# Transposed contexts from DRAM for the last layer, and the transpose of the router's shares a turn later

## The chip, the cores and the metric

The kernel runs on one NeuronCore of a Trainium2 chip. The metric is the device time of one execution in microseconds (us), the median of several runs; lower is better. The core has five engines with instruction queues of their own: TensorE (PE) multiplies matrices and transposes tiles into PSUM; VectorE (DVE), ScalarE (ACT) and GpSimd (POOL) work element by element; SyncE (SP) issues nearly all DMAs here. Everything is float32.

## The reference

A sequence of four layers on `x` of shape (128, 64, 128): 128 batches of 64 tokens with 128 channels. `cond` has one row of 128 for each batch, and `ctx` has the shape of `x`.

```
x = L0(x, cond, ctx)   # self attention, cross attention to ctx, MLP
x = L1(x, ctx, cond)   # cross attention to a normed ctx
x = L2(x, cond, ctx)   # self attention, cross attention to a normed ctx, MLP
x = L3(x, cond, ctx)   # one-head attention to ctx, then three experts with a router
```

All attention has 16 heads of width 8, except that of layer 3:

```
# L0, cross attention: the context enters without a norm
k, v = split(ctx @ kv_w + kv_b)
x = x + attend(ln(x) @ q_w + q_b, k, v) @ ca_proj_w + ca_proj_b

# L3
nx = layer_norm(x, gamma, beta)
weights = softmax((nx @ Wq) @ (ctx @ Wk).T * 128 ** -0.5)
evidence = weights @ (ctx @ Wv)
combined = concat(nx, evidence, anchor)              # anchor: cond, the same for all tokens of a batch
probs = softmax(combined @ router_W + router_b)      # three experts
h = silu(combined @ e_w1[e] + e_b1[e])               # e = 0, 1, 2
routed = sum_e probs[e] * (h @ e_w2[e] + e_b2[e])
g = sigmoid(silu(combined @ gate_w1 + gate_b1) @ gate_w2 + gate_b2)
out = x + g * (routed @ out_w + out_b)
```

Two places of it bear on the change: the cross attention of layer 0 and layer 3 both need the raw context with channels on the partitions, that is, transposed.

## The kernel before, in words

**Tiling.** The 8192 tokens are cut into 16 groups (`NST`) of 512, eight batches each. A group of `x` is a tile of 128 partitions by 4 by 128 (`xs[s]`) and stays in SBUF throughout. A transposed group is a tile of 128 channels by 512 tokens, made by `transposed`: four PE transposes of 128x128 into one PSUM bank (L296), which ACT or DVE then copies to SBUF.

**Stages.** Five attentions over 16 groups each make 80 items, run in two pipelines (`attend`): first L0's self and cross attention, then L1's and L2's two. An MLP stage (`mlp`) follows each pipeline, and layer 3 (`layer_3`) ends the kernel. The order on every engine is the order in which the program is written out: `tc.manual_schedule()`. Each engine, SP's queue too, works strictly in that order. Neighbouring stages overlap: the last steps of one and the first "heads" of the next are called in turn.

**One item of attention.** `prepare` is a generator in eight pieces. For cross attention they are: load the context `c` (L345), statistics of `x`, norm, transposed context `cm` (L332, in L0 a plain ACT copy of the transposes), transposed `x`, keys (with POOL's `kbd`), queries, values. `scores`, `turned` and `weighted` make the attention in halves. `finish` has four pieces:

- the sums of the softmax go from the tile `o` to DRAM (`sums`, L486) and back in another shape (`rc`, L491), and half of `o` is moved to other partitions (L494)
- DVE takes the reciprocal (L496); it goes to DRAM (`recs`, L498) and comes back spread over the partitions (`rb`, L500)
- POOL multiplies: `oT` (L503), and adds a bias to `x`
- PE projects: `py` (L509), and DVE adds it to `x`

In one step, the context's transposes of an item are written just ahead of the second piece of `finish` of the item four places earlier, so that on SP a DMA issued with them stands just ahead of `recs`.

**Layer 3.** The products of the weights that don't depend on the data are made beside the MLP of layer 2. Each group then passes these functions: `load` (the context `c` and the statistics), `norm` (POOL), `nx` (transposes and affine), `context` (transposed context `cT`), `queries` and `score`, `weights` (ACT's exponential, DVE's sum and reciprocal, POOL's product into `pd`, L914), `turn_weights` (transposes of `pd`), `evidence`, `router`, `logits`, `shares` (softmax over the experts, `pr`, L962), `turn_shares` (one PE transpose of `pr`, L968, and ACT's copy `prT`, L970), seven times `hidden` (two matmuls each, L980 and L981), `gate`, four times `output`, one for each 128 tokens (L1012; L1015 uses `prT`), and `store`.

A turn `a` does the hidden layers of group `a`, while groups `a + 1` and `a + 2` come nearer and `a - 1` is finished. The turn's list is its order. Four places matter:

- it starts with `norm`, then `hidden(a, 6)`, then `turn_weights(a + 1)`
- `router(a + 1)` comes after `hidden(a, 3)`, and `queries(a + 2)` after `hidden(a, 4)`
- it ends with `output(a, 0)`, `shares(a + 1)`, `weights(a + 2)`, `turn_shares(a + 1)`
- `output(a, 1)` to `output(a, 3)` run in the next turn

Ahead of the turns lie seven heads, called between the last turns of the MLP, and a `bridge` that brings group 0's shares. Router, logits and shares use one PSUM buffer in turn (`ps`). The tiles `cT` and `acc` of layer 3 lie in the buffers of `cm` and `y`, two each.

Of the kernel before, what the change touches and what calls it, by code (L numbers as in the profile page):

```python
# [9 lines left out]
F32 = mybir.dt.float32  # L10
AF = mybir.ActivationFunctionType
ALU = mybir.AluOpType
# [3 lines left out]
P = 128  # L16
NST = 16
# [3 lines left out]
NT = TT * P  # L21
# [38 lines left out]
def tile_kernel(ctx: ExitStack, tc: tile.TileContext, a: dict, out: bass.AP):  # L60
    nc = tc.nc
    V, S, G, T = nc.vector, nc.scalar, nc.gpsimd, nc.tensor
# [3 lines left out]
    def const(shape, name):  # L66
        return cp.tile(shape, F32, tag=name, name=name)
# [3 lines left out]
    out_d = out.rearrange("b n c -> (b n) c").rearrange("(s t p) c -> s p t c", t=TT, p=P)  # L71
# [21 lines left out]
    xs = [const([P, TT, P], f"x{s}") for s in range(NST)]  # L93
# [16 lines left out]
    for name, n in (("L0_xcond_ca_proj_b", P), ("L1_xcond_bp", P), ("L2_xcond_b_cproj", P), ("L3_xcond_router_b", 3)):  # L110
        t = const([P, n], name)
# [11 lines left out]
    dp = ctx.enter_context(tc.tile_pool(name="dp", bufs=1, space=bass.MemoryType.DRAM))  # L123
# [163 lines left out]
    def stats_of(pool, src, eps):  # L287
        mv = pool.tile([P, TT, 2], F32, tag="mv", name="mv")
        stats(pool, src, mv)
        return mv, inv_std(pool, mv, eps)  # L290

    def transposed(psum, src):

        ps = psum.tile([P, 512], F32, tag="mm", name="psT")
        for t in range(TT):
            T.transpose(ps[:, ts(t, P)], src[:, t, :], ident)  # L296
        return ps

    def modulated(pool, ps, name, scale, shift, s, tag="xm"):
        xm = pool.tile([P, NT], F32, tag=tag, name=tag)  # L300
        V.tensor_tensor(by_batch(xm), by_batch(ps), mod(name, scale, s), ALU.mult)
        G.tensor_tensor(by_batch(xm), by_batch(xm), mod(name, shift, s), ALU.add)
        return xm
# [16 lines left out]
    def normed_by_pool(pool, src, mv, rs, tag):  # L320
        nmu = pool.tile([P, TT], F32, tag="nmu" + tag, name="nmu")
        G.tensor_scalar(nmu, mv[:, :, 0], -1.0, 0.0, ALU.mult, ALU.add)
        xn = pool.tile([P, TT, P], F32, tag=tag, name=tag)
        for t in range(TT):
            G.tensor_scalar(  # L325
                xn[:, t, :], src[:, t, :], nmu[:, t : t + 1], rs[:, t : t + 1], ALU.add, ALU.mult
            )
        return xn

    def copied(pool, ps, tag):  # L330
        t = pool.tile([P, NT], F32, tag=tag, name=tag)
        S.copy(t, ps)  # L332
        return t

    turn = [0]

    def prepare(pools, at):

        pool, psum = pools[:2]
        s, layer = at["s"], at["layer"]  # L340
        eps = 1e-5 if layer == "L1c" else 1e-6
        cross = layer[2] == "c"
        if cross:
            c = pool.tile([P, TT, P], F32, tag="c", name="c", bufs=3)
            nc.sync.dma_start(c, ctx_d[s])  # L345
        yield
        mv, rs = stats_of(pool, xs[s], eps)
        yield
        xn = normed_by_pool(pool, xs[s], mv, rs, "xn")
        if cross:  # L350
            cn = c
            if layer != "L0c":
                cn = pool.tile([P, TT, P], F32, tag="cn", name="cn", bufs=1)
                for t in range(TT):
                    S.activation(
                        cn[:, t, :], c[:, t, :], AF.Identity,
                        bias=ctx_nb[eps][:, s, t : t + 1], scale=ctx_rs[eps][:, s, t : t + 1],
                    )
        yield
        if layer == "L1c":  # L360
            kv_in = modulated_by_act(pool, transposed(psum, cn), "L1_xcond_Wss_kv", 0, 1, s, "cm")
        elif cross:
            kv_in = copied(pool, transposed(psum, cn), "cm")
        else:
            q_in = kv_in = modulated_by_act(pool, transposed(psum, xn), at["wmod"], 1, 0, s)
        yield
        if not cross:
            pass
        elif layer == "L1c":
            q_in = modulated(pool, transposed(psum, xn), "L1_xcond_Wss_q", 0, 1, s)  # L370
        else:
            q_in = copied(pool, transposed(psum, xn), "xm")
        yield


        pk = psum.tile([P, 512], F32, tag="mm", name="pk")
        T.matmul(pk, at["wk"], kv_in, start=True, stop=True)  # L377
        kT = pool.tile([P, NT], F32, tag="kT", name="kT")
        S.activation(kT, pk, AF.Identity, bias=at["bk"])  # L379
        i = turn[0] % 2  # L380
        turn[0] += 1
        vbd = vbds[i]
        kbd = pool.tile([P, 4, NB, L], F32, tag="kbd", name="kbd")
        for j in range(4):
            G.tensor_scalar(  # L385
                kbd[:, j], by_batch(kT), mask[:, j : j + 1], 1.0, ALU.mult, ALU.mult
            )
        yield
        pq = psum.tile([P, 512], F32, tag="mm", name="pq")
        T.matmul(pq, at["wq"], q_in, start=True, stop=True)  # L390
        qT = pool.tile([P, NT], F32, tag="qT", name="qT")
        S.activation(qT, pq, AF.Identity, bias=at["bq"])
        yield

        wv_pair = at["wv"].rearrange("p (i j d) -> p j i d", j=2, d=HD)
        pvv = psum.tile([P, NB, L], F32, tag="mm", name="pvv")
        for b in range(NB):
            for j in range(2):
                T.matmul(  # L399
                    pvv[ts(j, L), b, :], kv_in[:, ts(b, L)], wv_pair[:, j],  # L400
                    start=True, stop=True,
                )
        pv4 = pvv.rearrange("p b (i d) -> p b i d", d=HD)
        S.copy(vbd[0:L, :, :, 0:HD], pv4[0:L])
        S.copy(vbd[L:P, :, :, HD : 2 * HD], pv4[L:P])
        at.update(qT=qT, kbd=kbd, vbd=vbd)
# [445 lines left out]
    def layer_3():  # L852

        pmm = pools[1]
# [6 lines left out]
        def sb(shape, tag, bufs=2):  # L861
            of = pools[0] if tag in shared else l3_pool[0]
            return of.tile(shape, F32, tag=shared.get(tag, tag), name=tag, bufs=bufs)
# [5 lines left out]
            d["mv"], d["rs"] = stats_of(l3_pool[0], xs[s], 1e-5)  # L869

        def norm(d):
            d["xn"] = normed_by_pool(l3_pool[0], xs[d["s"]], d["mv"], d["rs"], "xn")

        def nx(d):
# [3 lines left out]
                d["nx"], ps, AF.Identity, bias=col("L3_xcond_ln_beta"),  # L878
                scale=col("L3_xcond_ln_gamma"),
            )  # L880

        def context(d):
            ps = transposed(pmm, d["c"])
            d["cT"] = sb([P, NT], "cT")
            S.copy(d["cT"], ps)

        def queries(d):
            ps = mm("pq")
# [132 lines left out]
                )  # L1021
            V.tensor_add(acc, po[:, 3, :], acc)  # L1022

        def store(d):
            acc = d["acc"]
            G.tensor_tensor(acc, acc, d["g"], ALU.mult)  # L1026
            G.tensor_tensor(acc, acc, xs[d["s"]], ALU.add)
            nc.sync.dma_start(out_d[d["s"]], acc)

        ds = [dict(s=s) for s in range(NST)]  # L1030

        def go(f, j, *more):
            if 0 <= j < NST:
                f(ds[j], *more)

        heads = [
            lambda: (go(load, 0), go(load, 1)),
            lambda: go(norm, 0),
            lambda: (go(nx, 0), go(context, 0), go(norm, 1)),
            lambda: (go(queries, 0), go(score, 0), go(load, 2)),  # L1040
            lambda: (go(weights, 0), go(nx, 1), go(context, 1), go(norm, 2)),
            lambda: (go(turn_weights, 0), go(queries, 1), go(score, 1)),
            lambda: (go(evidence, 0), go(load, 3)),
        ]
# [1 line left out]
        def bridge():  # L1046
            go(router, 0)
            go(weights, 1)
            go(logits, 0)
            go(shares, 0)  # L1050
            go(turn_shares, 0)

        def turn(a_):
            b_, c_ = a_ + 1, a_ + 2
            return [
                lambda: go(norm, c_ + 1),
                lambda: go(hidden, a_, 6),
                lambda: go(turn_weights, b_),
                lambda: go(output, a_ - 1, 1),
                lambda: go(hidden, a_, 0),  # L1060
                lambda: go(nx, c_),
                lambda: go(output, a_ - 1, 2),
                lambda: go(hidden, a_, 1),
                lambda: go(evidence, b_),
                lambda: go(output, a_ - 1, 3),
                lambda: go(store, a_ - 1),
                lambda: go(hidden, a_, 2),
                lambda: go(context, c_),
                lambda: go(hidden, a_, 3),
                lambda: go(router, b_),  # L1070
                lambda: go(hidden, a_, 4),
                lambda: go(queries, c_),
                lambda: go(hidden, a_, 5),
                lambda: go(logits, b_),
                lambda: go(score, c_),
                lambda: go(load, c_ + 2),
                lambda: go(gate, a_),
                lambda: go(output, a_, 0),
                lambda: go(shares, b_),
                lambda: go(weights, c_),  # L1080
                lambda: go(turn_shares, b_),
            ]

        return heads, bridge, [turn(j) for j in range(NST + 1)]
# [127 lines left out]
```

## Time and profile before

| | |
|---|---|
| time, median of three runs | 1814.87 us (1810.33 to 1819.31) |
| profiled execution: its own time | 1817.44 us |
| profiled execution: span of the instructions | 1815.7 us, mean granted clock of TensorE 0.975 |
| first pipeline (L0's attentions) | up to about 460 us |
| second pipeline (L1, L2) | about 570 to 1230 us |
| layer 3's turns | from 1350 us |
| from 1350 us to the end: PE, DVE, ACT, POOL busy | 407.4, 196.7, 188.7, 108.5 of 466 us, granted clock 0.93 |
| from 265 to 400 us (L0's cross attention): the same | 133.6, 121.8, 96.3, 92.7 of 135 us, granted clock 0.99 |

How to read it. The page gives busy times of each engine and, in 40 slices, its busy share in tenths; the row PEclk is the share of its full clock that PE was granted. In the waits, a row says which engine and line waited for which, for how long in all, how often, and the longest. In the timeline a row has the start and the length in us, engine, line, operation, tiles written and read, and in brackets the idle time before it and what ended it. In the windows a row has the stretch, its length, the busy time of PE, PE's weight loads, DVE, ACT and POOL with the number of instructions, then the granted clock, the share of the DMA engines and GB/s.

### The profile page before, as it was taken

To read this page: it belongs to the slowest core of one execution; us is meant where nothing else is said; L and a number is where in the kernel's file an instruction comes from. 1 tells how busy PE (TensorE), PEld (TensorE's weight loads), DVE (VectorE), ACT (ScalarE), POOL (GpSimd) and SP (SyncE) were. 2 spreads that over 40 slices of the span, in tenths; PEclk is the share of its full clock that TensorE was granted. 3 is DMA by queue.
4 is the path that set the end of the run, shared out by engine and by line. 5 is a ranking of instruction groups with operands and counts; after the bars stand their busy time and mean duration, and the time that the engine had idled before them with its cause. 6 is when DMAs were issued, how large, how long until landed. Compare 5 with 4: busy or idle time off the path is not lost. (4 is left out here: it accounts for less than half of the span.)

```text
span 1815.7 us, 64689 instructions
## 1 busy us (share of the span) xinstructions
PE 1648.6 (91%) x27756; PEld 1097.2 (60%) x27756; DVE 1248.5 (69%) x2281; ACT 1085.2 (60%) x1864; POOL 1028.0 (57%) x1671
## 2 busy tenths in 40 slices
PE   5999899998999888899998899989998989898987
PEld 3666567775444666676666677755545656555555
DVE  4899789996545888899898899964534344444443
ACT  4877667775335877778777788853344344444443
POOL 5677676666888566677777666666522222222211
PEclk9999999999999999999999999999999899899999
DMA  7233332221111122113333322111000000000000
GB/s 201 63 84 90 89 90 63 64 55 51 42 56 29 36 54 57 46 46 83 82 89 98 83 64 69 52 43 55 1 6 18 13 24 15 21 24 13 18 7 18
DMA packets 149949, 95.78 MB, mean 53 GB/s; under 512 B 35301, under 2 KB 132511, under 8 KB 149663
## 3 DMA queue, kind: packets, MB, share of 16 engines
q1 hardware_dynamic: 148874, 91.42, 18.4%
q8 instruction: 218, 3.57, 0.8%
q14 instruction: 68, 0.56, 0.1%
q10 hardware_dynamic: 789, 0.23, 0.1%
HBM read 71.41 MB, written 9.70 MB: 45 GB/s over the span
## 5 line engine op out<-in xcount | busy, mean ns | idle before, releaser
L425 DVE TENSOR_REDUCE mx<-sc 128x32 f32<-128x2048 f32 x160 | 365.9, 2287 | 81.0 <-PE sc L418 80.9
L447 ACT ACTIVATE eT<-pp 128x1024 f32<-128x1024 f32 x320 | 330.2, 1032 | 110.2 <-PE pp L443 110.2
L427 DVE TENSOR_TENSOR e<-sc,mx 128x2048 f32<-128x2048 f32 x160 | 366.6, 2291 | 5.5
L443 PEld LDWEIGHTS pp<-ident,e 64*128 64x128 f32 x5120 | 185.9, 140 | 202.4 <-issue 82.0
L385 POOL TENSOR_SCALAR kbd<-kT,mask 128x512 f32<-128x512 f32 x320 | 214.9, 690 | 59.8 <-ACT kT L379 59.2
L443 PE MATMUL pp<-ident,e 64*128 64x64 f32 x5120 | 230.0, 230 | 19.7 <-ACT eT L447 14.4
L325 POOL TENSOR_SCALAR xn<-x,nmu,rs 128x128 f32<-128x128 f32 x512 | 221.7, 446 | 13.4
L418 PE MATMUL sc<-kbd,qT 32*64 32x256 f32 x5120 | 181.1, 390 | 21.7 <-DVE e L427 20.2
L635 ACT ACTIVATE h<-ph,vec 128x512 f32<-128x512 f32 x128 | 87.3, 687 | 162.7 <-PE ph L634 162.5
L503 POOL TENSOR_TENSOR oT<-o,rb 128x512 f32<-128x512 f32 x80 | 101.8, 1273 | 145.2 <-DMA sums<-o 31.6
L460 PE MATMUL po<-eT,vbd 128*32 128x64 f32 x10240 | 176.9, 221 | 0.0
L987 ACT ACTIVATE h<-h 128x512 f32<-128x512 f32 x112 | 70.5, 630 | 168.2 <-DVE h L983 149.3
L983 DVE TENSOR_TENSOR h<-ph,ab 128x512 f32<-128x512 f32 x112 | 77.3, 690 | 133.6 <-PE ph L981 133.3
L460 PEld LDWEIGHTS po<-eT,vbd 128*32 128x32 f32 x10240 | 151.0, 110 | 12.2 <-DVE mv L276 0.8
L284 POOL TENSOR_TENSOR rs<-rs,nhalf 128x4 f32<-128x4 f32 x128 | 130.2, 1017 | 10.7
L418 PEld LDWEIGHTS sc<-kbd,qT 32*64 32x64 f32 x5120 | 98.3, 132 | 57.5 <-issue 33.7
L1019 DVE SCALAR_TENSOR_TENSOR acc<-po,pr,acc 128x128 f32<-128x128 f32 x128 | 44.9, 351 | 115.2 <-ACT acc L1017 112.9
L1026 POOL TENSOR_TENSOR acc<-acc,g 128x512 f32<-128x512 f32 x16 | 20.3, 1268 | 181.8 <-DVE acc L1022 135.5
L379 ACT ACTIVATE kT<-pk,vec 128x512 f32<-128x512 f32 x80 | 55.0, 687 | 111.1 <-PE pk L377 111.1
L283 POOL TENSOR_SCALAR rs<-mv 128x4 f32<-128x4 f32 x128 | 25.3, 198 | 156.5 <-DVE mv L276 142.2
L468 ACT COPY o<-po 128x512 f32<-128x512 f32 x160 | 95.5, 597 | 24.9 <-POOL oT L503 11.0
L274 DVE BATCH_NORM_STATS2 st<-x 128x6 f32<-128x128 f32 x512 | 110.3, 278 | 0.0
(257 smaller groups left out, 3109.9 us busy)
## 6 DMA issues: line engine op xcount, KB each, us to landing
rb<-recs SPq DMA_DIRECT2D x80, 256.0 KB
c<-in_ctx_dram SPq DMA_DIRECT2D x80, 256.0 KB
o<-o SPq DMA_DIRECT2D x320, 32.0 KB
gt<-gate_L_xcond_sa_proj_w SPq DMA_DIRECT2D x64, 128.0 KB
gt<-gate_L_xcond_W_proj SPq DMA_DIRECT2D x64, 128.0 KB
sums<-o SPq DMA_DIRECT2D x320, 8.0 KB
x<-in_x_dram SPq DMA_DIRECT2D x16, 256.0 KB
out_dram<-acc SPq DMA_DIRECT2D x16, 256.0 KB
```

The lines of the kernel that those rows point to most:

```text
L274: V.bn_stats(st[:, t, :], src[:, t, :])
L284: G.tensor_tensor(rs, rs, nhalf, ALU.pow)
L325: G.tensor_scalar(xn[:, t, :], src[:, t, :], nmu[:, t : t + 1], rs[:, t : t + 1], ALU.add, ALU.mult)
L385: G.tensor_scalar(kbd[:, j], by_batch(kT), mask[:, j : j + 1], 1.0, ALU.mult, ALU.mult)
L418: T.matmul(sc[ts(h, L), g, ts(t2, 256)], qT[ts(g, 32), ts(b, L)], kbd[ts(g, 32), :, b, :], start=True, stop=True,)
L425: V.tensor_reduce(mx, sc.rearrange("p g (m k) -> p (g m) k", k=L), AX.X, ALU.max)
L427: V.tensor_tensor(e, sc.rearrange("p g (m k) -> p (g m) k", k=L), mx.unsqueeze(2).broadcast_to([P, 32, L]), ALU.subtract,)
L443: T.transpose(pp[:, h, ts(4 * g2 + 2 * i + t2, L)], e6[ts(h, L), 2 * gg + g2, t2, i], ident[ts(h, L), ts(h, L)],)
L447: S.activation(eT[:, gg], pp, AF.Exp, scale=HD ** -0.5)
L460: T.matmul(po[ts(g, 32), i, ts(2 * t2 + h, L)], at["vbd"][:, 4 * u + 2 * t2 + h, 2 * g + i, :], e7[:, g // 2, h, g % 2, i, t2, :], start=T ...
L468: S.copy(at["o"][:, :, ts(u, 256)], po)
L503: G.tensor_tensor(oT, o[:, 0, :], rb, ALU.mult)
```

## The change

There are four parts.

- In L0's cross attention, right after ACT has copied the transposed context to `cm`, SP stores that tile in DRAM (`ctxT`), once for each of the 16 groups.
- In layer 3 `context`, with its transposes and copy, is gone. `norm` loads the tile `cT` from `ctxT` instead, nearly two turns ahead of its use in `score`.
- `turn_shares` of a group moves from the end of one turn into the middle of the next, after `hidden(a, 4)`; it leaves the bridge too.
- `store` is gone. Each `output` multiplies by the gate and adds `x` for its own 128 tokens on POOL, and every second one stores two parts.

```diff
@@ tile_kernel
+
+    ctxT = dp.tile([NST, P, NT], F32, tag="ctxT", name="ctxT")
@@ prepare
         elif cross:
             kv_in = copied(pool, transposed(psum, cn), "cm")
+            if layer == "L0c":
+                nc.sync.dma_start(ctxT[s], kv_in)
@@ layer_3
         def norm(d):
+            d["cT"] = sb([P, NT], "cT")
+            nc.sync.dma_start(d["cT"], ctxT[d["s"]])
             d["xn"] = normed_by_pool(l3_pool[0], xs[d["s"]], d["mv"], d["rs"], "xn")
...
-        def context(d):
-            ps = transposed(pmm, d["c"])
-            d["cT"] = sb([P, NT], "cT")
-            S.copy(d["cT"], ps)
...
             V.tensor_add(acc, po[:, 3, :], acc)
 
-        def store(d):
-            acc = d["acc"]
-            G.tensor_tensor(acc, acc, d["g"], ALU.mult)
-            G.tensor_tensor(acc, acc, xs[d["s"]], ALU.add)
-            nc.sync.dma_start(out_d[d["s"]], acc)
+            G.tensor_tensor(acc, acc, d["g"][:, t, :], ALU.mult)
+            G.tensor_tensor(acc, acc, xs[d["s"]][:, t, :], ALU.add)
+            if t % 2:
+                two = slice(t - 1, t + 1)
+                nc.sync.dma_start(out_d[d["s"]][:, two, :], d["acc"][:, two, :])
@@ heads
-            lambda: (go(nx, 0), go(context, 0), go(norm, 1)),
+            lambda: (go(nx, 0), go(norm, 1)),
             lambda: (go(queries, 0), go(score, 0), go(load, 2)),
-            lambda: (go(weights, 0), go(nx, 1), go(context, 1), go(norm, 2)),
+            lambda: (go(weights, 0), go(nx, 1), go(norm, 2)),
@@ bridge
             go(shares, 0)
-            go(turn_shares, 0)
@@ turn
                 lambda: go(output, a_ - 1, 3),
-                lambda: go(store, a_ - 1),
                 lambda: go(hidden, a_, 2),
-                lambda: go(context, c_),
                 lambda: go(hidden, a_, 3),
                 lambda: go(router, b_),
                 lambda: go(hidden, a_, 4),
+                lambda: go(turn_shares, a_),
                 lambda: go(queries, c_),
...
                 lambda: go(shares, b_),
                 lambda: go(weights, c_),
-                lambda: go(turn_shares, b_),
```

## The prediction

> **What bounds the kernel now.** I read the page's first two parts, then the waits of TensorE (PE) in the last layer, then the timeline of one turn of that layer on each engine, then the granted clock in 3.41 us stretches, and last the DMA queue of SyncE (SP) in the first cross attention, because that is where the change adds work.
>
> ```profile
> PE 1648.6 (91%) x27756; PEld 1097.2 (60%) x27756; DVE 1248.5 (69%) x2281; ACT 1085.2 (60%) x1864; POOL 1028.0 (57%) x1671
> PEclk9999999999999999999999999999999899899999
> ```
>
> PE is the bound nearly everywhere. The clock row dips only in the last quarter, from about 1350 us: layer 3. The waits of PE from 1345 us to the end name one cause:
>
> ```profile
> PE pp L968 <- DVE pr L962: 50.1, 16, 3.4
> ```
>
> That is `turn_shares`, 16 times: 1.8 us in the bridge, about 3.4 in each turn, 2.7 in the last three. The timeline around one of them, PE first and then POOL:
>
> ```profile
> 1578.89 0.39 PE L1015 MATMUL po<-b_2o,prT 128*128 128x128 f32 x2
> 1582.61 0.45 PE L968 MATMUL pp<-ident,pr 128*128 128x128 f32 x1 [3.33 <-DVE pr L962]
> 1582.85 1.92 PE L980 MATMUL ph<-nx,L_xcond_gate_w 128*128 128x512 f32 x2
> 1584.55 1.91 PE L981 MATMUL ph<-u,w_gev 128*128 128x512 f32 x2
> 1586.26 1.06 PE L296 MATMUL psT<-ident,pd 128*128 128x128 f32 x4
> ...
> 1583.15 1.29 POOL L914 TENSOR_TENSOR pd<-e,sm 64x256 f32<-64x256 f32 x2 [2.22 <-DVE sm L909]
> ```
>
> See the last line: `pd`, which PE turns right after `hidden 6`, is ready only at 1584.44, 1.9 us after the shares. So behind the stall that the change removes stands a second one, now covered by `hidden 6` (L980 and L981, 1.72 us at full clock).
>
> ```profile
> 1349.71:1353.12 3.41, 1.23 (x18) 0.58 (x8) 2.12 (x9) 0.43 (x2) 1.75 (x4) 1.00 0.00 0
> 1353.12:1356.53 3.41, 3.41 (x8) 1.73 (x7) 0.58 (x1) 1.33 (x2) 1.40 (x4) 0.50 0.00 0
> ...
> 1779.79:1783.20 3.41, 1.33 (x4) 0.74 (x5) 1.33 (x6) 1.57 (x3) 0.00 (x0) 1.00 0.00 0
> 1783.20:1786.61 3.41, 3.41 (x14) 2.71 (x13) 0.69 (x1) 1.36 (x2) 0.00 (x0) 0.50 0.00 0
> ```
>
> After a stretch in which PE was busy 1.23 or 1.33 of 3.41 us, the next stretch ran at clock 0.50, and costs 1.7 us of work. All changes of the clock in this trace lie on one grid of 3.41 us; stretches 46% busy or less were followed by half clock, one 50% busy was not, and it returned after stretches at least 79% busy.
>
> SP's queue in the first cross attention, and once just before it:
>
> ```profile
> 197.59 0.59 SPq L345 DMA_DIRECT2D c<-in_ctx_dram  x1
> 198.23 0.50 SPq L498 DMA_DIRECT2D recs<-rc  x1
> 202.71 0.56 SPq L500 DMA_DIRECT2D rb<-recs  x1
> ...
> 305.01 0.34 SPq L498 DMA_DIRECT2D recs<-rc  x1
> 307.04 0.56 SPq L500 DMA_DIRECT2D rb<-recs  x1
> ```
>
> `recs` alone lands within 1.5 to 2.6 us (mean 1.8 in this stage; `rb` is issued as soon as it lands); directly behind a 256 KB load of `c` it took 4.4 us.
>
> **The change, part by part.** The sum is made against the profiled execution, 1817.44 us (span 1815.7); the median of the runs is 1814.87, 2.6 lower, and I move the difference over to it.
>
> *Contexts of groups 0 and 1, in the MLP before.* Each removes four transposes and a PE wait for a PSUM buffer: PE finished the turn of `xn` at 1303.5 and began the next matmul of the MLP at 1304.71. 1.2 us each in a stage 97% PE: 2.4 us. The two ACT copies were hidden and give nothing. The new loads of `cT` are issued two heads (some 10 us) ahead of `score`; a 256 KB load lands in about 3 us, so they stay hidden, and without that cover would cost 3 us once.
>
> *The bridge.* Without `turn_shares(0)`, `hidden 6` starts at 1350.6 in place of 1352.70: 2.1 us. The stretch to 1353.12 is then busy, so the half clock after it goes: 1.7. `pd` of group 1 is ready at 1352.39, before PE gets there. Together 3.8 us.
>
> *Turns 0 to 13.* The period at full clock is 27.6 us: 29.0 from the shares at 1377.62 to those at 1406.62, less 1.4 lost while PE worked at half clock until 1380.4. New: PE goes straight on to `hidden 6`, finishes it 1.72 us after `output 0`, and waits for `pd`. From `pd`'s turn to the end of `hidden 5` is 18.99 us now (1380.86 to 1399.85), 0.44 less for the context's four transposes and 0.13 more for the moved one: 18.68. From there to `pd` ready is 8.6 (1399.85 to 1408.5): ACT and DVE in their own order (max, `e`, the statistics of a later group, `g`, tanh, a table load of 1.28, two exponentials, sum, reciprocal, then POOL), none of which the change shortens. 27.28, so 0.3 less. The stall is 3.5 us where it was 3.35, so the clock still falls. I laid the 14 stalls of both kernels on the 3.41 us grid with the bounds above, over all starting phases: the new ones come out 2 to 8 us shorter in all. I take 4.
>
> *The end of turn 14.* No `pd` follows there, so this stall is really gone: 2.7, the transpose 0.1, and the half clock from 1783.20, 1.7: 4.6 us (4.5 to be cautious).
>
> *The tail.* The last group's two POOL operations take 1.26 each over 512 columns after the last DVE operation; L914 takes 0.61 for 256, so 128 columns are about 0.33. 2.6 becomes 0.75; the last store is half as large. 2.0 us. In other turns the pairs of short POOL operations fit: after `output 0` they run from about 1581.5 to 1582.3, before `pd` may start at 1583.15. SP's 16 additional stores wait only for POOL; behind them stand loads needed a turn later.
>
> *The moved transpose.* Its PSUM buffer is single; the router's result in it is read (L941, 1571.48 to 1571.76) while PE is in `hidden 4` until 1573.2, so PE finds it free. ACT's copy (0.27) goes ahead of that of `qT`, which `score` needs 1 us later. Nothing.
>
> *The stores of `ctxT` in the first cross attention.* 16 DMAs of 256 KB. On SP each stands just ahead of `recs` of an earlier group, and waits for ACT's copy `cm`, which ends with the reciprocal (305.01 and 304.99), so that wait itself is free; what pays is the queue. Behind it: `recs`, `rb`, then POOL's `oT` (L503), behind which POOL holds later work, then PE's `py` (L509). The slack from the end of `oT` to `py` in the 16 groups concerned is 0.06, 1.04, 0.05, 0.06, 2.89, 1.91, 1.71, 1.44, 1.57, 0.79, 1.33, 1.79, 0.95, 1.76, 0.62, 1.07 us; what exceeds it stops PE, which is 99% busy there. For the delay D there is no row of this transfer. Lower end: its issue alone, 0.4 us (a row of the same size for the last store), costs 1 us in all. Upper end: as behind a load of `c`, `recs` 3.4 us on average and 0.6 of issue, so D = 2.2, costs 17. I take 1.1: a 256 KB store of the output lands 2.4 us after its issue, and `recs` then some 0.5 later. The excess over the slacks is 1.04, 0.06, 1.05, 1.04, 0.31, 0.15, 0.48 and 0.03: 4.2, say 4.5 us.
>
> [...]
>
> [...]
>
> Sum: 2.4 + 3.8 + 4 + 4.5 + 2.0 = 16.7 gained, 4.5 paid: 12 us. 1817.4 becomes 1805.2; from the median, 1803.
>
> **The rivals.** *The queue costs more than the turns give.* One mechanism: `recs` waits behind the store as behind a load. At D = 2.2 gain and cost cancel (1815); from D = 2.8, 26 us of excess, the kernel is over 0.5% slower; at 3.25, the worst `recs` behind a `c`, it pays 33 and ends at 1831. For it: the first four groups have next to no slack but one. Against: the store has fewer and longer pieces than a load of `c`, and writes of 256 KB land sooner (2.4 against 3.1). 0.23, of which slower 0.09.
>
> *The clock stays up.* A stall of 3.5 us that falls evenly over two stretches leaves both 48% busy, between the bounds, and 27.28 us is close to 8 stretches, so it could repeat. Some 12 turns times 1.75 is 21 more: 1782. It needs a lucky phase: 0.09.
>
> *The stall vanishes*, as if `pd` weren't behind it: 50 us and all half clocks, about 25, with the transposes: about 1735. Against: `pd` at 1584.44. 0.02.
>
> **How the numbers follow.** My case has 0.66, by itself 1796 to 1811. A measurement of this kernel can tell about 0.5%, 9 us, from no change. Faster by more: most of my case, the clock and the vanished stall: 0.60. Within: the rest of my case and the queue up to D = 2.8: 0.31. Slower 0.09. The range reaches from 1789, below which lie most of the clock's case and the vanished stall (0.1), to 1818, above which lies what is left of the queue's (0.1).
>
> **What would show it.** Right: PE's wait for `pr` gone, in its place 14 waits of about 3.5 us for POOL's `pd` at L296 and half clock still about 0.93 in layer 3; no stall at the bridge and after turn 14; `recs` landing in 2.5 to 3 us where `ctxT` is stored, and PE waits at `py` of 4 to 5 us more. Wrong: periods of layer 3 well under 28.5 us, or a longer period than 12.19 us in the first cross attention.

## The result, and the profile after

| | before | after |
|---|---|---|
| median of nine runs | 1814.87 us (1810.33 to 1829.28) | 1805.96 us (1800.42 to 1810.18) |
| ratio, after to before | | 0.9947 (95%: 0.9925 to 0.9969) |
| profiled execution, its own time | 1817.44 us | 1801.63 us |
| its span, mean granted clock | 1815.7 us, 0.975 | 1799.7 us, 0.983 |

The changed kernel is 0.53% faster, 9.6 us by the ratio. The forecast was 1803. The sum came out, but two of its terms were wrong, in opposite directions, and what a part of the change is worth turned out to depend on the parts beside it. Most of what follows is about that.

The page after, its first line and the clock:

```profile
PE 1629.3 (91%) x27692; PEld 1086.8 (60%) x27692; DVE 1249.6 (69%) x2281; ACT 1078.8 (60%) x1848; POOL 1046.3 (58%) x1767
PEclk9999999999999999999999999999999999999999
```

PE is 19 us less busy, though the 64 transposes that are gone take only 7 (four take 0.44); the rest is work that no longer runs at half clock (what half clock costs, taken as half of PE's busy time at it, since the two pairs of `hidden 6` start 1.70 us apart there and 0.86 apart at full clock, goes from 39.2 us in the whole trace to 26.5). The dips of the clock row in the last quarter are gone in tenths, not in fact, as the turns below show. First PE's waits in layer 3 (who waited for whom, us in all, times, longest), and two parts of PE's timeline there, the bridge and the end of a turn:

```profile
PE psT L296 <- POOL pd L915: 49.5, 14, 3.7
```

```profile
1354.59 0.33 PE L949 MATMUL pl<-ident,lgT 128*128 128x128 f32 x1 [0.42 <-DVE lgT L942]
1354.76 1.02 PE L981 MATMUL ph<-nx,L_xcond_gate_w 128*128 128x512 f32 x2
...
1576.28 0.39 PE L1016 MATMUL po<-b_2o,prT 128*128 128x128 f32 x2
1576.51 1.02 PE L981 MATMUL ph<-nx,L_xcond_gate_w 128*128 128x512 f32 x2
1577.37 1.02 PE L982 MATMUL ph<-u,w_gev 128*128 128x512 f32 x2
1581.99 1.11 PE L296 MATMUL psT<-ident,pd 128*128 128x128 f32 x4 [3.60 <-POOL pd L915]
```

Set this beside the lines of before. 16 waits for `pr`, 50.1 us in all, have become 14 waits for `pd`, 49.5 us in all. The bridge goes from the logits (L949) straight to `hidden 6` (L981). At the end of a turn PE also goes straight on, now at full clock (1.02 for a pair where it was 1.92), and stands behind it for 3.60 us. The stall has moved by two matmuls and is no shorter.

Next three successive turns, from `output 0` to `output 0` (stretch, length, busy time and instructions of PE, weight loads, DVE, ACT, POOL, then the granted clock, DMA share, GB/s):

```profile
1547.19:1576.28 29.09, 25.49 (x146) 16.49 (x145) 12.65 (x39) 11.66 (x21) 8.62 (x18) 0.94 0.09 28
1576.28:1605.10 28.82, 25.22 (x146) 16.80 (x145) 12.66 (x39) 11.77 (x21) 8.62 (x18) 0.94 0.10 28
1605.10:1632.52 27.42, 23.82 (x146) 15.40 (x145) 12.66 (x39) 11.66 (x21) 8.63 (x18) 1.00 0.10 30
```

The same 146 instructions take 25.5, 25.2 and 23.8 us of PE. Two turns lose 1.7 and 1.4 us to half clock, the third loses none, and so it goes on: 29.09 + 28.82 + 27.42 = 85.33 = 25 x 3.413 us. The turns keep step with the grid of 3.413 us on which the clock changes: the 29 changes in this trace lie on one such grid within 3 ns, and so do the 43 in the trace of before. Here it is around the three stalls:

```profile
1547.40:1550.81 3.41, 1.90 (x6) 0.59 (x4) 1.86 (x8) 2.69 (x5) 2.54 (x5) 1.00 0.00 0
1550.81:1554.23 3.42, 1.33 (x12) 1.33 (x13) 1.14 (x4) 2.15 (x3) 2.44 (x7) 1.00 0.01 2
1554.23:1557.64 3.41, 3.41 (x11) 2.38 (x11) 0.99 (x3) 0.60 (x2) 0.98 (x3) 0.50 0.00 0
...
1578.12:1581.53 3.41, 0.27 (x1) 0.00 (x0) 2.35 (x8) 1.79 (x4) 1.92 (x5) 1.00 0.00 0
1581.53:1584.94 3.41, 2.95 (x14) 2.95 (x15) 0.00 (x0) 2.12 (x3) 2.33 (x6) 0.50 0.00 0
...
1605.42:1608.83 3.41, 1.78 (x5) 0.48 (x3) 1.86 (x8) 2.69 (x5) 2.54 (x4) 1.00 0.00 0
1608.83:1612.25 3.42, 1.44 (x13) 1.44 (x14) 1.03 (x3) 2.27 (x3) 2.52 (x6) 1.00 0.00 0
1612.25:1615.66 3.41, 3.41 (x21) 2.40 (x21) 1.69 (x4) 0.58 (x3) 1.54 (x4) 1.00 0.01 2
```

In the first stall a stretch with PE busy 1.90 us is followed by full clock, one with 1.33 by half. The second lies nearly whole in one stretch (0.27 busy), and half clock follows. The third splits into 1.78 and 1.44, and the clock stays up. Three stalls of one length, three phases, two outcomes.

Last, SP's queue in the first cross attention, where the store stands just ahead of `recs`:

```profile
329.97 0.34 SPq L367 DMA_DIRECT2D ctxT<-cm  x1
330.35 0.44 SPq L502 DMA_DIRECT2D recs<-rc  x1
333.76 0.57 SPq L504 DMA_DIRECT2D rb<-recs  x1
```

`rb` is issued when `recs` has landed: 3.4 us after its issue here, one of the slower ones. From the end of the reciprocal `rc` to the issue of `rb` it is 3.64 us on average over items 16 to 27 (the twelve of the first cross attention whose `recs` stand behind a store) where it was 2.01. The 1.63 us have two parts. `recs` is issued 1.02 us after the reciprocal (0.08 before), since SP waits until ACT's copy `cm` is done (it issues the store 0.64 us after the reciprocal) and then spends 0.38 on the store. And `rb` follows 2.62 us after the issue of `recs` (1.93 before). PE's waits in that stage (205 to 440 us), before and after:

```profile
PE py L509 <- POOL oT L503: 7.4, 5, 2.5
```

```profile
PE py L513 <- POOL oT L507: 13.1, 10, 3.2
```

**Where the 15.8 us of the two profiled executions lie.** By the stretches of the traces: heads and bridge, from the last `py` of the second pipeline to the first `output 0`, 140.0 to 133.5 (-6.5); the thirteen periods from the first `output 0` on 380.4 to 370.8 (-9.6); turns 14 and 15 48.38 to 44.07 (-4.3); from there to the end 13.06 to 10.92 (-2.1). Layer 3 with its heads gains 22.5. Everything before is 6.6 longer.

That 6.6 is not all the store. The stage from item 31 to item 79, whose code is the same in all the kernels, takes 760.0 to 767.8 us in the fourteen profiled executions of this case, and 761.5 and 767.8 in these two. The cost of the store is read better from many kernels. From item 11 to item 28 of the first cross attention, four profiled kernels with the store where the change puts it (the changed one and three below) take 222.1, 218.5, 225.4 and 226.6, mean 223.2; seven without it take 210.9 to 215.4 (before itself), mean 213.0. It costs about 10 us, of which the pair of before and after shows 6.7. 22.5 less 10 is 12.5, and the medians say 9.6 with an interval from 5.6 to 13.6.

### The profile page after: what moved, and what is told of

It is laid out like the page before. It is cut to its first block, busy times and chain, and to the rows that moved or that the text cites. A ratio compares the mean times of both kernels' runs of the same rounds, so it can differ in the third digit from the quotient of the medians.

```text
span 1799.7 us, 64744 instructions
## 1 busy us (share of the span) xinstructions
PE 1629.3 (91%) x27692; PEld 1086.8 (60%) x27692; DVE 1249.6 (69%) x2281; ACT 1078.8 (60%) x1848; POOL 1046.3 (58%) x1767
## 5 line engine op out<-in xcount | busy, mean ns | idle before, releaser
L325 POOL TENSOR_SCALAR xn<-x,nmu,rs 128x128 f32<-128x128 f32 x512 | 222.1, 448 | 13.4
L464 PEld LDWEIGHTS po<-eT,vbd 128*32 128x32 f32 x10240 | 150.4, 110 | 12.2 <-DVE st L274 0.8
L1025 POOL TENSOR_TENSOR acc<-acc,g 128x128 f32<-128x128 f32 x64 | 29.1, 454 | 146.8 <-DVE acc L1023 140.6
```

Source lines behind the costliest of these rows:

```text
L325: G.tensor_scalar(xn[:, t, :], src[:, t, :], nmu[:, t : t + 1], rs[:, t : t + 1], ALU.add, ALU.mult)
L464: T.matmul(po[ts(g, 32), i, ts(2 * t2 + h, L)], at["vbd"][:, 4 * u + 2 * t2 + h, 2 * g + i, :], e7[:, g // 2, h, g % 2, i, t2, :], start=T ...
```

## The experiments

I started with the theory of the prediction: the gain is a sum of parts, each near its term. The rival was that the parts don't add, because the turns answer to the grid. After the first four runs, in which three kernels that should have been faster were slower, the rival became my theory, and the later runs test it. Kernels of one group ran on one chip with the same runs of before: the first four with a median of 1811.59, the next four 1817.83, the last four 1810.39. Ratios are compared, not times.

### One part alone, and three without one

**The shares' transpose alone**, in before:

```diff
             go(shares, 0)
-            go(turn_shares, 0)
...
                 lambda: go(hidden, a_, 4),
+                lambda: go(turn_shares, a_),
...
-                lambda: go(turn_shares, b_),
```

> The kernel before with the moved transpose of the shares alone. My theory (the stall moves to pd): the waits for pr (50 us) go, 14 waits of about 3.6 us for pd appear, a turn is not shorter (27.7 us at full clock against 27.6); only the bridge (3.8) and the end of turn 14 (4.5) are gained: 6 to 9 us faster than before. Rival (the stall was the cost): 50 us and the half clocks go, 60 us or more.

Measured: 1.0022 (1.0008 to 1.0037), slower. The mechanics are as foreseen: heads and bridge take 136.36, 3.6 less than before; turns 14 and 15 take 43.97, 4.4 less; and the wait has moved:

```profile
PE psT L296 <- POOL pd L914: 48.1, 14, 3.6
```

But the thirteen periods between are 12.4 us longer. The period at full clock (its length less half of the time in which PE worked at half clock, here and below the mean of the first twelve) is 27.68, against 27.53 before. That is 2 us in thirteen turns. The other 10 come from the clock: the loss in these turns is 33.5 us where it was 23.1, since nine of the thirteen periods take 30.50 to 30.73 us, close to nine stretches of 3.413 (30.72).

**The outputs' split alone**, in before:

```diff
-        def store(d):
-            ...
+            G.tensor_tensor(acc, acc, d["g"][:, t, :], ALU.mult)
+            G.tensor_tensor(acc, acc, xs[d["s"]][:, t, :], ALU.add)
+            if t % 2:
+                two = slice(t - 1, t + 1)
+                nc.sync.dma_start(out_d[d["s"]][:, two, :], d["acc"][:, two, :])
...
-                lambda: go(store, a_ - 1),
```

> The kernel before with the gate, the addition of x and the store in four and two parts alone. My theory: 2 us faster, all behind the last DVE operation. Rival (short POOL operations after output 0 hold up pd, or 16 more stores cost): no gain or slower, with layer 3's turns longer than 29.2 us on average.

Measured: 1.0027 (1.0012 to 1.0043), slower. The tail is 2.1 us shorter, as it should be. The turns are longer: 27.63 at full clock, 0.1 more. POOL's second operation ends beside DVE's `pr`; here both, and then the same `pr` before:

```profile
1587.51 0.45 POOL L1025 TENSOR_TENSOR acc<-acc,x 128x128 f32<-128x128 f32 x1
```

```profile
1587.71 0.28 DVE L962 TENSOR_TENSOR pr<-lg,ls 128x12 f32<-128x12 f32 x1
```

```profile
1582.29 0.17 DVE L962 TENSOR_TENSOR pr<-lg,ls 128x12 f32<-128x12 f32 x1
```

`pr` takes 0.28 us where it took 0.17, and ends 0.03 us after POOL's operation does (1587.99 and 1587.96). The same shows in a row of before: in the bridge `pr` runs beside POOL's `pd`, takes 0.51 us and ends at 1352.42, 0.03 us after it; the median of its 16 `pr` is 0.171. Why `pr` takes longer beside POOL is not shown. With the grid the 0.1 us becomes 0.3 a turn, 4.2 us in all, more than the tail gives.

**The contexts alone**, in before (the store of `ctxT`, the load of `cT`, no `context`):

```diff
             kv_in = copied(pool, transposed(psum, cn), "cm")
+            if layer == "L0c":
+                nc.sync.dma_start(ctxT[s], kv_in)
...
+            d["cT"] = sb([P, NT], "cT")
+            nc.sync.dma_start(d["cT"], ctxT[d["s"]])
...
-                lambda: go(context, c_),
```

> The kernel before with the contexts through DRAM alone. My theory: 2.4 us less in the heads, 0.44 less in each of 14 turns, 4.5 more in the first cross attention: 4 us faster in all; waits of PE for oT there rise by 4 to 7 us. Rival (the stores are hidden): 8 to 9 us faster and no more waits at py.

Measured: 0.9946 (0.9928 to 0.9964): alone as fast as the whole change. The period at full clock is 27.16, just under eight stretches (27.31), and several turns in a row keep the full clock:

```profile
1595.78:1622.99 27.21, 23.88 (x146) 15.48 (x145) 12.49 (x39) 11.62 (x21) 7.52 (x12) 1.00 0.11 30
1622.99:1650.20 27.21, 23.88 (x147) 15.48 (x145) 12.48 (x39) 11.62 (x21) 7.52 (x12) 1.00 0.11 30
```

**The change without the contexts** (shares and outputs in before):

> The changed kernel without the contexts through DRAM: moved shares and split outputs alone. My theory: 8 to 11 us faster than before, about the same as the changed kernel, since the contexts gain and pay nearly the same; first cross attention at 12.19 us an item. Rival (the contexts carry the change): 4 us faster at most.

Measured: 1.0033 (1.0022 to 1.0045), slower, although it has the gains at the bridge, after turn 14 and in the tail. From the third to the twelfth, the periods close in on nine stretches (30.49 to 30.72 us):

```profile
1605.00:1635.72 30.72, 27.11 (x151) 18.07 (x150) 12.68 (x39) 12.24 (x22) 8.62 (x18) 0.89 0.06 18
1635.72:1666.44 30.72, 27.11 (x151) 18.07 (x150) 12.68 (x39) 12.23 (x22) 8.61 (x18) 0.89 0.07 18
```

At full clock its period is 27.78, and the changed kernel's 27.38. The 0.4 us of four transposes lie between turns of 30.72 and a mean of 28.52; the next section tests that.

### Does the grid set the price of work in layer 3?

If so, more work may cost several times its own length in one kernel, and less than nothing in another. Four transposes whose result nobody reads go into each turn, first of the changed kernel, then of the last one above. They repeat those of `context`.

```diff
+        def extra(d):
+            transposed(pmm, d["c"])
...
                 lambda: go(hidden, a_, 2),
+                lambda: go(extra, c_),
```

> The changed kernel with four transposes more in each of 14 turns, whose result nobody reads: 0.44 us of PE work a turn, 6 us in all. Theory of the grid (layer 3's turns fall in step with the 3.41 us stretches of the clock, so their length is not the sum of their work): the turn at full clock goes from 27.4 to 27.8 us, and its measured length to that of the kernels with 27.7, 30.7 us with nearly 3 us lost each time: 20 to 28 us slower than the changed kernel, 10 to 18 slower than before. Rival (the sum of the work): 6 us slower than the changed kernel.

> The same four transposes more in the kernel of moved shares and split outputs without the contexts, whose turns stand at 30.72 us, nine stretches. Theory of the grid: the turn at full clock goes from 27.75 to 28.2 us, but its length stays at or under 30.7: from 14 us faster to no slower than that kernel (1.0033 of before), in spite of 6 us more work. Rival (the sum of the work): 6 us slower than that kernel, 1.0067 of before.

Measured: the changed kernel with them 1.0073 (1.0046 to 1.01) where it is 0.9947 without, 23 us more for about 6 us of transposes (in the traces the thirteen periods take 395.7 us in place of 370.8). The other, without contexts through DRAM, 1.0000 (0.998 to 1.0021) where it was 1.0033 (1.0022 to 1.0045). That is 6 us less, on another chip and with intervals that only just part; what is clear is that it isn't 6 us slower. Its thirteen periods take 386.1 us in place of 393.0. First a turn of the one, then two of the other:

```profile
1627.42:1658.14 30.72, 27.12 (x151) 18.07 (x150) 12.66 (x39) 11.76 (x21) 8.62 (x18) 0.89 0.10 26
```

```profile
1458.77:1488.72 29.95, 26.34 (x155) 17.61 (x153) 12.66 (x39) 12.12 (x22) 8.62 (x18) 0.94 0.06 18
1488.72:1517.02 28.30, 24.69 (x155) 16.23 (x153) 12.66 (x39) 12.13 (x22) 8.62 (x18) 1.00 0.07 19
```

The first takes 27.76 at full clock and locks to nine stretches. The second takes 28.26, too long for that lock, and some of its turns keep the full clock. With 146, 151 and 155 matmuls a turn takes 28.52 us on average, 30.72 once settled, and 29.70 on average (28.3 to 31.1): the time of these turns doesn't grow with their work. This decides for the grid and against the sum of parts.

### Taking the stall away

**The weights later**, in the changed kernel: `turn_weights` goes behind `output 2` of the group before and `evidence` behind its `output 3`, so that PE has work while `pd` is made.

```diff
                 lambda: go(hidden, a_, 6),
-                lambda: go(turn_weights, b_),
...
                 lambda: go(output, a_ - 1, 2),
+                lambda: go(turn_weights, b_),
                 lambda: go(output, a_ - 1, 3),
+                lambda: go(evidence, b_),
```

> The changed kernel with the transposes of pd three places later (after output 2) and evidence behind output 3. Theory (the stall is a wait for pd that other PE work of the turn can cover): the 14 waits of 3.6 us go, with them the half clock; turns of about 23.3 to 24 us: 60 to 70 us faster than the changed kernel, near 1740. Rival (ACT and DVE can't follow, a new wait takes its place): 0 to 20 us faster, with a wait of PE for pT, u or a PSUM buffer of over 2 us a turn.

Measured: 0.959 (0.9566 to 0.9613). A turn, and then all of layer 3:

```profile
1595.32:1619.00 23.68, 23.68 (x146) 15.60 (x145) 12.38 (x39) 11.40 (x21) 8.62 (x18) 1.00 0.11 34
1350.00:1741.00 391.00, 385.26 (x2290) 251.39 (x2289) 197.54 (x583) 183.22 (x334) 127.21 (x265) 1.00 0.10 29
```

PE is busy 385 of 391 us at full clock, and the largest group of waits there is 0.4 us. The changed kernel's stalls, 49.5 us, and its half clock, 15.4 us, are 65 us; 0.9947 less 0.959, of 1815, is 65 us.

**The same move alone**, in before:

> The kernel before with the transposes of pd moved behind output 2, as in the fastest version so far, and nothing else. Theory (two stalls stand one behind the other, the shares' at 6.9 us after hidden 5, pd's at 8.6, and only moving both helps): PE still waits 3.4 us for pr in every turn; the turn at full clock stays at 27.5 us, so within 6 us of before. Rival (pd's transposes were the stall): 40 us faster or more.

Measured: 0.9989 (0.9973 to 1.0004), no change:

```profile
PE pp L968 <- DVE pr L962: 50.0, 16, 3.4
```

The stall for `pr` hides the one for `pd`. Each of the two moves alone leaves 48 to 50 us of stall, both together, with the rest of the change, leave none.

### What the store of the contexts costs, and why

**The store one piece of `prepare` later**, behind `recs` and `rb` on SP, in the changed kernel:

```diff
-            if layer == "L0c":
-                nc.sync.dma_start(ctxT[s], kv_in)
...
         q_in = copied(pool, transposed(psum, xn), "xm")
+        if layer == "L0c":
+            nc.sync.dma_start(ctxT[s], kv_in)
```

> The changed kernel with the store of ctxT one piece of prepare later, so that on SP it stands behind recs and rb. Theory (recs is late behind the store): the waits of PE for oT in the first cross attention fall from 13 us back to about 6, an item there is 12.19 us again: 4 to 7 us faster than the changed kernel, 14 to 16 faster than before. Rival (the additional DMA traffic, wherever it stands, costs): the same as the changed kernel.

**The store in ACT's queue**, in the changed kernel:

```diff
-                nc.sync.dma_start(ctxT[s], kv_in)
+                nc.scalar.dma_start(ctxT[s], kv_in)
```

> The changed kernel with the store of ctxT issued from ACT's queue, at the same place of the program. Theory (recs is late for what stands ahead of it on SP's queue): PE's waits for oT in the first cross attention fall to about 6 us, as with the later store; 3 to 6 us faster than the changed kernel. Rival (the two transfers meet in the DMA engines whichever queue issues them): recs still lands a microsecond later than before, the waits stay near 13 us, no gain over the changed kernel.

Measured: 0.9918 (0.9894 to 0.9942) and 0.9912 (0.9883 to 0.9942), where the changed kernel has 0.9947. The intervals overlap, so the totals alone don't show a gain. The stage shows one. From `rc` to `rb` it is 2.07 and 2.15 us again (before 2.01, after 3.64), items 11 to 28 take 217.7 and 213.0 (with the store ahead of `recs` 223.2 on average, without a store 213.0), and PE's waits are

```profile
PE py L513 <- POOL oT L507: 9.2, 6, 2.8
```

```profile
PE py L513 <- POOL oT L507: 6.4, 5, 2.6
```

for the later store and for ACT's queue. With the later store 217.7 us, and 215.7 in the kernel of the next section that has it too, stay above the 210.9 to 215.4 of the kernels without a store; whether it still costs something is not shown. In ACT's queue (q10, 4.43 MB there and 0.23 before) the same 16 stores of 256 KB cost nothing that the stage shows. So what delayed `recs` was its place behind the store in SP's queue, not the 256 KB as such. Both parts of the delay go: `recs` is issued 0.03 us after the reciprocal, and `rb` follows 2.12 us later (2.62 behind the store, 1.93 before).

### Both, and what is left of the contexts

**Weights later and store later**, in the changed kernel:

> The changed kernel with the transposes of pd behind output 2 and the store of ctxT one piece of prepare later. Theory (the two costs add now that layer 3 has no stall): 4 to 6 us less than with the transposes alone (0.959 of before): 0.956, about 1738. Rival (the store's place showed only through the phase of the clock in layer 3): the same 0.959.

Measured: 0.9537 (0.9509 to 0.9565), median 1727.25 us, 83 us below before on the same chip and the fastest of all these kernels. By the ratios that is 10 us less than with the weights alone, more than the 4 to 6 expected; the two ran on different chips and their intervals only just part.

**Weights later without contexts through DRAM** (shares and outputs kept):

> The version with the transposes of pd behind output 2, without the contexts through DRAM: what the contexts are worth where the clock stays full. Theory (they save 0.44 us in each of 14 turns and 2.4 in the heads and cost 4 to 6 in the first cross attention): 2 to 5 us slower than with them, 0.960 to 0.962 of before. Rival (they carry 10 us, as they did alone): 0.965.

Measured: 0.9563 (0.9535 to 0.9592); a turn takes 24.12 us, 0.44 more than with the contexts through DRAM (23.68), as the four transposes cost. Yet, against the expectation, it is not slower than the kernel with the store ahead of `recs` (0.959): that store takes about 10 us and the contexts give about 9 (14 times 0.44, and nearly 3 in the heads: 6.5 less the bridge's 3.6). Against the one with the later store (0.9537) the contexts may give 5 us, but the intervals overlap. Whether the contexts through DRAM pay once the stall is gone stays open.

## Why the prediction was right, and where its terms were not

- **The stall moves from `pr` to `pd` and stays as long.** Right, and the most useful step: 14 waits of 3.5 us were foretold, 14 with a mean of 3.54 came (49.5 / 14). It rested on one line, the `pd` at 1584.44 behind the stall. The two kernels with the weights later show both halves of it.
- **Heads and bridge, 6.2.** Right: 6.5. The bridge alone gave 3.6 of the 3.8 foretold.
- **Turns 0 to 13, 4 from a span of 2 to 8.** Too small: 9.6. The period at full clock was nearly right, 27.53 to 27.38 where I had 27.6 to 27.28 (the 0.1 between 27.38 and 27.28 is the pair on POOL, below). What failed is the value taken for the clock: I let the starting phase decide within 2 to 8 us. In the traces the turns fall into a pattern and keep it. Before repeats every five turns in 43 stretches, after every three in 25; the loss in thirteen turns is 23.1 us before and 15.4 after. The 7.7 between them and 13 x 0.15 = 2.0 make the 9.6. The rival "the clock stays up" has come true in every third turn.
- **The end of turn 14 and the tail, 4.5 and 2.0.** Right: 4.3 and 2.1.
- **The short pairs on POOL, nothing.** Wrong in the kernel of before, as the outputs' split alone shows: one operation takes 0.45 us, not 0.33, and beside the second `pr` takes 0.28 in place of 0.17. Wrong in the changed kernel too. There PE no longer waits for `pr`, but `pr` takes 0.28 us as well, and behind it on DVE stand the sum and the reciprocal that `pd` waits for. With the shares moved and the outputs whole, the 14 waits for `pd` are 48.1 us and the period at full clock is 27.68; with the outputs split as well, 49.5 and 27.78: 0.1 us a turn.
- **The stores of `ctxT`, 4.5.** Too small: about 10. The place was right, the size was not: the delay is 1.6 us where I took 1.1. Two steps failed. I put SP's wait for `cm` at nothing, since in the row of before it ends with the reciprocal; in the changed kernel SP issues the store 0.64 us after the reciprocal on average, 0.05 to 0.12 in six of the twelve items and 0.46 to 2.86 in the others. And with the store's issue, `recs` then goes out 0.94 us later than before, to which 0.69 of later landing come. The later landing shows in the packets of the trace: in all 16 items the last packet of `recs` ends 0.12 to 1.19 us after the last of the store, which ends 1.69 to 3.09 us after the store's issue. (The store has 128 packets of 2 KB, a load of `c` 512 of 512 bytes.) What orders the two is not shown. With 1.6 in the place of 1.1 my list of 16 slacks gives 8.6 us, so the list was sound. The sign named for a miss came true: where before goes from `py` to `py` in 12.2 to 12.3 us from item 16 to item 27, five of these items now take 12.7 to 13.9. Not settled: PE's waits at `py` are 13.0 us on average in the four kernels with the store there and 5.2 in the seven without one, a growth of 7.8 us where the stage grew by 10. Why `cm` comes later is open too.
- **The bounds of the clock.** Softer than the prediction took them. 1.33 us of work in 3.41 (39%) were followed by half clock, as foreseen, but 1.44 (42%) kept the full clock, where the prediction had 46% followed by half clock. Busy time in the profile alone doesn't decide it.

So 16.7 became 22.5 and 4.5 became 10; the errors of 5.8 and 5.5 cancelled. The forecast named the right size by luck in good part: with four transposes more, at a period of 27.76, the same kernel was slower than before (1.0073).

## What to carry to other kernels

Look behind the stall that you remove for the next thing that is late: here two waits stood one behind the other, each move alone left about 50 us, and the second of them took 65 us off the changed kernel, which had the first. Where a loop keeps a stall of about the length of the clock's grid, as here (3.5 and 3.41 us), its time need not be the sum of its work (6 us of it cost 23 in one kernel and nothing in another); don't tune it by tenths, take the stall away first. A transfer that nobody waits for soon can still delay what stands behind it in its queue, 1.6 us here: issue it behind the urgent ones, or in another queue.

## What was not expected of the hardware

- The turns lock to the grid of 3.413 us: 30.72 us (nine stretches) in three kernels with periods at full clock of 27.68 to 27.78, 85.33 (25) for three turns of the changed kernel, and 27.2 (nearly eight) for several turns of the one with the contexts alone. 6 us of transposes cost 23 us in one kernel and nothing, or less, in another.
- A 256 KB store directly ahead of a small one in a queue delayed what follows by 1.6 us, 0.9 of it before the small one was issued; the same store in another queue delayed it by about 0.1 (2.15 against 2.01 us).
- A short DVE operation (`pr`) took 0.28 in place of 0.17 us beside a POOL operation, and ended 0.03 us after it.
- Open: what besides PE's busy time decides the clock (1.44 us of 3.41 kept it full, 1.56 before did not); whether each run of a kernel falls into the same pattern, since one execution of each was profiled (the mean granted clock speaks for it: 0.968 to 0.975 in all 22 runs of the change without the contexts, 0.978 to 0.983 in the nine of the changed kernel, 0.976 to 0.981 in the 13 of the kernel with 155 matmuls); and the causes of the 8 us by which a stage of unchanged code differs among profiled executions.
